# A hyperbolic transformer block on one core: one period per quad, joint scalar chains, tiles placed by the planner, one-bank PSUM tiles, other bias products

## The chip, the cores and the metric

One core of a Trainium2 chip. The metric is the device time of one launch in microseconds, median of the runs. Engines are named as in the profile: PE (TensorE), DVE (VectorE), ACT (ScalarE), POOL (GpSimd) and SP (SyncE, which here issues every DMA).

## The reference, cut to what matters

x is 128 x 64 x 256 in float32, cond is 128 x 256. A block of hyperbolic attention and a hyperbolic MLP are applied to x and the result is added to x. log0 and exp0 scale a row by a function of its norm; plin is exp0(log0(x) @ w + b).

```python
ada = t_emb @ w_ada + b_ada
sh_msa, sc_msa, g_msa, sh_mlp, sc_mlp, g_mlp = jnp.split(ada, 6, axis=-1)
xm = expmap0(layer_norm(logmap0(x)) * (1 + sc_msa) + sh_msa)
q = _to_heads(plin(xm, w_q, b_q))          # k, v alike; 16 heads of 16
attn = softmax(logmap0(q) @ logmap0(k).T / sqrt(HD))
attn_out = plin(_from_heads(expmap0(attn @ logmap0(v))), w_o, b_o)
x1 = mobius_add(x, expmap0(g_msa * logmap0(attn_out)))
xm = expmap0(layer_norm(logmap0(x1)) * (1 + sc_mlp) + sh_mlp)
ff = plin(plin(xm, w_f1, b_f1), w_f2, b_f2)
out = x + mobius_add(x1, expmap0(g_mlp * logmap0(ff)))
```

## The kernel before, in words

The 8192 rows are 64 tiles of 128 rows; four tiles are a quad, two a pair. Since log0 and exp0 only scale rows, the kernel never forms them: it carries rows and, per row, scalar factors, which are worked out on small tiles of 4, 8 or 16 columns (`norm_scalars`, `mobius_scalars`, `clip_factor`, `rsqrt_core`, L563 to L679): a long chain of tiny DVE operations with a few ACT logarithms and exponentials in between. The two MLP products have no activation between them, so `load_rest` (L748) folds the weights once into `wm`, two 256 x 256 blocks: f1 times f2 ("hw"), and f1 times its own transpose ("hm"), which gives the norm of the hidden row.

*Attention* (L983) runs over the quads of a group. `modulated` (L809) scales rows (on ACT or DVE, whichever is free), multiplies by the condition's scale on DVE, adds its shift on POOL (L819), and sums squares on ACT. `transposed` (L827) turns the rows on PE and spreads the inverse norms across partitions with four more transposes. `attention_pair` (L857) then takes a pair: q, k, v products (L868), bias products with one-row operands (L874), squares (L878) and their sums by head (L880), factors, scaled u and ve (L900, L904), transposes of u, qx and kT (L920, L924), 32 score products, exponentials in two pieces of 1024 columns (L936), 128 value products, division, transposes, and the product with wo (L976), whose bias comes as a full 128 x 512 product (L977). `gated` (L845) multiplies by the gate and sums squares and dot products. At the end of the group `mobius_scalars` works out two factors per row, a and b, and x1 = a x + b p is formed by one ACT or POOL and one DVE operation per tile (L1005, L1006).

*The MLP* (L1010) does the same for a group's quads: statistics, scalars, `modulated`, `transposed`, hm and hw, `fm` = hw times a factor plus b2 on DVE (L1062), `gated`, `mobius_scalars`, and the output with x added (L1076, L1077), stored per quad.

*The order of the work.* Groups are [0], [1, 2], ..., [13, 14], [15]: two quads share one run of each scalar chain. Nothing is issued as it is written: each operation goes into a `Plan` with an engine (or a choice, "ACT/DVE"), a modelled duration and a key: the quad's number for attention, plus `LAG` = 3.5 for its MLP (L1103). `Plan.run` (L150) sorts out an order by key and readiness, with its own durations, and `issue` writes it down; each engine then runs its list in that order. A DVE operation with SBUF inputs alone isn't picked while POOL is taken to be busy (L214). Where PE would have nothing to do, filler products of the identity are put in (`warm`, L1082). PSUM is two one-bank tiles ("bank") and three two-bank tiles ("dbl"). Row statistics of later quads are taken in four batches from x loaded for that alone (`passing`, L1096).

SP's queue issues all DMAs: x, the condition's scale, shift and gate rows per pair (written to DRAM once, read back with each row repeated 64 times), xr (x again, for the last addition) and the output.

## Time and profile before

| what | value |
|---|---|
| median of 3 runs | 911.72 us (911.11 to 917.18) |
| profiled execution, span | 919.3 us (its own time; no separate time of it is listed) |
| mean granted TensorE clock | 0.905 |
| PE, DVE, ACT, POOL busy | 814.0, 724.2, 501.6, 97.1 us |
| instructions | 24167 |
| DMA | 92.14 MB, mean 100 GB/s |
| first and last q product of attention | 27.55 us and 776.62 us from the span's start |

The page's first part gives each engine's busy time over the span, the second the same in 40 slices of 23 us. A table of stretches gives busy time by engine, the granted clock and DMA for any piece of the span. A group's line gives engine, operation, tiles (without numbers), shape and count, then busy time, mean length of one in ns, and the idle time ahead of it with what ended it. A float32 product is two matmul records, a transpose one. An engine starts an operation before the last one's record has ended, so a mean is some 0.08 to 0.11 us longer than the spacing of such operations in a dense run, and the groups' busy times add up to more than the engine's.

### The profile page before, as it was taken

What the parts mean: (1) busy time and instruction counts of PE and PEld (TensorE: products, weight loads), DVE (VectorE), ACT (ScalarE), POOL (GpSimd) and SP (SyncE); (2) the same over time, 40 slices, a digit from 0 to 9 for tenths busy, and PEclk for the clock granted to TensorE, in tenths of its full rate; (3) what the DMA queues carried; (4) which work ended last, traced back from release to release, by engine and by line L of the source; (5) the groups of instructions that cost most, each with busy time, mean ns of one, the idle gap of its engine ahead of it and who ended that gap; (6) DMA issues with size and microseconds to landing.
All of it is one profiled execution on the core that took longest, in us unless ns stands there. A gap on an engine that the chain in (4) does not pass through costs nothing.

```text
span 919.3 us, 24167 instructions
## 1 busy us (share of the span) xinstructions
PE 814.0 (89%) x9236; PEld 577.4 (63%) x9236; DVE 724.2 (79%) x2923; ACT 501.6 (55%) x1480; POOL 97.1 (11%) x91
## 2 busy tenths in 40 slices
PE   7888889898897988899879996999699959998996
PEld 5463556566676756676557764776477636766666
DVE  5567698758868997499966988689957996689877
ACT  2143455537765765457754774557646655555432
POOL 0002111000211111012010112021110111011200
PEclk9979979899989996799897996899879989999988
DMA  6886524102422425114441336024421251002413
GB/s 184 264 241 170 145 86 121 50 13 81 129 80 71 128 80 149 48 49 126 128 115 33 108 81 184 14 77 126 139 64 31 70 155 49 25 24 83 126 53 109
DMA packets 77268, 92.14 MB, mean 100 GB/s; under 512 B 7136, under 2 KB 59232, under 8 KB 77152
## 3 DMA queue, kind: packets, MB, share of 16 engines
q1 hardware_dynamic: 77152, 90.60, 34.8%
q8 instruction: 72, 1.18, 0.5%
q14 instruction: 44, 0.36, 0.1%
HBM read 81.40 MB, written 9.18 MB: 99 GB/s over the span
## 4 chain that ended last, share of the span: by engine, by line
PE 42%; DVE 29%; ACT 13%; issue 9%; DMA 5%; POOL 1%; SPq 1%; DVEq 0%; POOLq 0%; ACTq 0%
PE hmm L432 8%; PE ava L432 6%; PE wpa L432 5%; PE qka L432 5%; PE hwm L432 5%; PE tqa L436 3%; PE vva L432 3%; PE sca L432 2%; DVE bx L382 2%; DVE hs L395 2%; DVE p L382 2%; DVE ua L372 2%; PE wt L1084 1%; PE tza L436 1%; DMA mdm<-ada_d 1%
## 5 line engine op out<-in xcount | busy, mean ns | idle before, releaser
L432 PE MATMUL qka<-wqkv,yTa 128*128 128x512 f32 x256 | 144.6, 648 | 3.0 <-DVE maden L372 2.2
L432 PEld LDWEIGHTS vva<-wqkv,yTa 128*128 128x128 f32 x256 | 51.5, 203 | 72.9 <-issue 62.6
L432 PEld LDWEIGHTS ava<-ve,pta 64*64 64x64 f32 x4096 | 75.9, 157 | 18.4 <-issue 6.0
L432 PE MATMUL vva<-wqkv,yTa 128*128 128x256 f32 x256 | 81.0, 400 | 3.0 <-DVE n1st L410 1.5
L432 PE MATMUL ava<-ve,pta 64*64 64x17 f32 x4096 | 79.3, 223 | 1.8 <-issue 1.7
L1084 PE MATMUL wt<-ident 128*128 128x128 f32 x388 | 68.4, 322 | 5.0 <-ACT j1a L420 3.2
L432 PE MATMUL hmm<-wm,yTm 128*128 128x256 f32 x256 | 69.2, 417 | 1.1 <-ACT yTm L406 1.1
L432 PE MATMUL wpa<-wo,zTa 128*128 128x256 f32 x256 | 64.8, 398 | 5.2 <-ACT zTa L406 5.0
L420 ACT ACTIVATE usqa<-qka 128x1024 f32<-128x1024 f32 x32 | 32.4, 1014 | 67.2 <-PE vva L432 59.2
L436 PE MATMUL tqa<-ident,ua 128*128 128x128 f32 x256 | 44.1, 326 | 27.5 <-DVE ua L372 22.5
L1084 PEld LDWEIGHTS wt<-ident 128*128 128x128 f32 x388 | 57.2, 204 | 17.3 <-PE wt L1084 8.8
L420 ACT ACTIVATE qxa<-tqa,par 128x512 f32<-128x512 f32 x64 | 43.7, 687 | 43.0 <-PE tqa L436 31.0
L420 ACT ACTIVATE pta<-sca 128x1024 f32<-128x1024 f32 x64 | 62.6, 1019 | 8.2 <-PE sca L432 8.2
L375 POOL TENSOR_TENSOR ym<-ym,mdm 128x512 f32<-128x512 f32 x31 | 41.9, 1358 | 231.1 <-DVE ym L372 120.9
L432 PE MATMUL hwm<-wm,yTm 128*128 128x256 f32 x256 | 63.4, 390 | 0.0
L375 POOL TENSOR_TENSOR ya<-ya,mda 128x512 f32<-128x512 f32 x30 | 40.5, 1359 | 206.1 <-DVE ya L372 95.4
L432 PE MATMUL sca<-qxa,kTa 32*64 32x128 f32 x2048 | 44.5, 300 | 17.9 <-DVE ua L372 7.1
L432 PEld LDWEIGHTS hmm<-wm,yTm 128*128 128x128 f32 x256 | 50.0, 205 | 14.9 <-issue 6.9
L432 PEld LDWEIGHTS qka<-wqkv,yTa 128*128 128x128 f32 x256 | 50.6, 208 | 13.0 <-issue 4.1
L432 PEld LDWEIGHTS wpa<-wo,zTa 128*128 128x128 f32 x256 | 47.5, 196 | 15.9 <-ACT zTa L406 5.9
L436 PEld LDWEIGHTS tqa<-ident,ua 128*128 128x128 f32 x256 | 35.3, 167 | 31.9 <-issue 16.8
L432 PEld LDWEIGHTS hwm<-wm,yTm 128*128 128x128 f32 x256 | 46.2, 189 | 13.5 <-issue 8.4
(278 smaller groups left out, 1783.3 us busy)
## 6 DMA issues: line engine op xcount, KB each, us to landing
mda<-ada_d SPq DMA_DIRECT2D x64, 256.0 KB, 4.3
mdm<-ada_d SPq DMA_DIRECT2D x64, 256.0 KB, 4.1
x<-in_x_dram SPq DMA_DIRECT2D x16, 512.0 KB, 3.9
xr<-in_x_dram SPq DMA_DIRECT2D x32, 256.0 KB, 3.4
gaa<-ada_d SPq DMA_DIRECT2D x64, 128.0 KB, 3.1
gmm<-ada_d SPq DMA_DIRECT2D x64, 128.0 KB, 3.0
out_dram<-p SPq DMA_DIRECT2D x16, 512.0 KB, 3.8
xp<-in_x_dram SPq DMA_DIRECT2D x30, 256.0 KB, 3.3
```

The lines of the kernel that those rows point to most:

```text
L372: fn = lambda: self.nc.vector.tensor_tensor(out, a, b, op)
L375: fn2 = lambda: self.nc.gpsimd.tensor_tensor(out, a, b, op)
L382: fn = lambda: self.nc.vector.scalar_tensor_tensor(out, a, s, b, op0, op1, **({} if accum is None else {"accum_out": accum}))
L395: fn = lambda: self.nc.vector.tensor_reduce(out, a, AX.X, ALU.add)
L420: fn = lambda: self.nc.scalar.activation(out, a, func, scale=scale, **kw)
L432: fn = lambda: self.nc.tensor.matmul(out, lhsT=lhsT, rhs=rhs, start=start, stop=stop)
L436: self.add([("PE", lambda: self.nc.tensor.transpose(out, a, ident), 0.112, 0.2, False)], [a, ident], [out])
L1084: nc.tensor.matmul(wt[:, 0:P], lhsT=ident, rhs=ident, start=True, stop=True)
```

## The change

The kernel is written anew around the same arithmetic.

- One quad is the unit. `joined(q)` works out one Mobius chain of 8 columns for the attention of quad q and the MLP of quad q-2; `norms(q)` one normalisation chain for the MLP of quad q and the attention of quad q+3, whose x is loaded then and kept, so the loads for the statistics alone go.
- Every stage of a quad has a name, and its key is the quad's number times a step plus an offset from a table of about 130 (`OFF`). The planner, `arrange`, has other durations and also chooses the place of every tile (`SLOTS` lists tags and how many places each has). Every operation has one engine: all copies out of PSUM, the first normalisation scale and half of the x1 update go to ACT; POOL adds all shifts but the first quad's, multiplies by the scale in attention (half of the multiplications) and takes the rest of the x1 update, so x1 is ACT (b times p), POOL (a times x) and POOL (sum); the last quad's sum stays on DVE.
- PSUM is eight one-bank tiles: q/k per tile of rows, four score tiles with exponentials of 512 columns, two value tiles.
- Bias products: the inverse norms sit in one transposable tile, so a stage needs one transpose for them, not four; q/k and v biases are products with 4-row operands ahead of the main products, three to a pair; the MLP's are two of 512 columns with 4 rows (hm) and, for hw with b2, two with 8 rows, which replaces `fm`: hw's factor `ft` is put into the scalars instead. The bias of wo is four 128 x 128 transposes of a broadcast column.
- hm uses the symmetry of its weights: the second half of the rows is multiplied into 128 columns only, with a doubled block.
- At the start, weights of the MLP and x of quads 0 to 4 are loaded ahead of the condition, and the weights are folded before the first attention; quad 0 takes scale and shift by a selecting product (`pick`), without the trip through DRAM.

The diff, cut to its core:

```diff
-    GROUPS = [[0]] + [[q, q + 1] for q in range(1, NQ - 1, 2)] + [[NQ - 1]]
-    def bank(name):
-        return pl.tile(ps, [P, 512], "bank", name, 2, space="psum")
-    def dbl(name):
-        return pl.tile(ps, [P, 1024], "dbl", name, 3, space="psum")
+    pl.tag("bank", 8, (P, 512), ps, False)
+SLOTS = [
+    ("x", 5, (1024,)), ("ya", 3, (512,)), ("ym", 4, (512,)), ("mda", 2, (1024,)), ("mdm", 2, (1024,)),
...
+X1_ACT, OUT_POOL, MUL_POOL = (0, 1, 2, 3), (), ("a0", "a1")
+OFF = {
+    "asq1": -202327, "mmul1": -198589, "a1za0": -177714, "a0hsv": -160580, "x": -157317, "xr": -153864,
...
+STEP = 37000
+def key_of(name, q):
+    return q * STEP + OFF.get(name, 0)
...
+    def side(self, products, reserve=()):
...
+            for out, lhsT, rhs, start, stop in products:
+                self.nc.tensor.matmul(v(out), lhsT=v(lhsT), rhs=v(rhs), start=start, stop=stop)
...
     def modulated
-            pl.ts(y[:, t, :], src[:, t, :], s[:, t : t + 1], o[:, t : t + 1], ALU.mult, ALU.add, eng="ACT/DVE")
-            pl.tt(y[:, hs_, :], y[:, hs_, :], md[:, :, D : 2 * D], ALU.mult)
-            pl.tt(y[:, hs_, :], y[:, hs_, :], md[:, :, 0:D], ALU.add, eng="DVE/POOL" if i0 < 4 else "POOL")
+                pl.ts(y[:, t], src[:, k], s[:, k : k + 1], o[:, k : k + 1], ALU.mult, ALU.add, eng=ACT)
+                pl.tt(y, y, md[:, :, D : 2 * D], ALU.mult, eng=POOL if m + str(r) in MUL_POOL and q else DVE)
+                pl.tt(y, y, md[:, :, 0:D], ALU.add, eng=POOL if q else DVE)
...
     def attention_pair
-                (0, qk, 0, 0, 512, True), (1, qk, 32, 0, 512, True), (0, vv, 64, 512, 768, False), (1, vv, 64, 512, 768, True)
-                pl.mm(o_[:, t], rT[r : r + 1, t0 + t, :], bqkv[r : r + 1, n0:n1_], False, stop)
+        pl.side(
+            [(qk[t], rT[32 * t : 32 * t + 4], brow[32 * t : 32 * t + 4, t0 + t], True, False) for t in range(2)]
+            + [(vv.flat(), rT[64:68], brow[64:68].flat()[:, t0 * D : (t0 + 2) * D], True, False)],
...
-        pl.copy(kT.rearrange("p t f s -> p (t f s)"), tq[:, 512:1024], eng="DVE/ACT")
+        pl.copy(kT.flat(), tk.flat(), eng=ACT)
...
-            pl.mm(wps.rearrange("p t d -> p (t d)"), first, bo, False, True)
+                    pl.mm(wps[:, t, c * P : (c + 1) * P], boc[:, c : c + 1].wide(0, P)[:, :, 0], ident, t == c == 0, False, True)
...
+    def joined(q):
...
+        a, b = mobius_scalars(x2, wp, xpd, "mo", fts.get(q - 2), lo)
...
-            pl.ts(ax, x_q[:, i % 4, :], a[:, i : i + 1], None, ALU.mult, eng="ACT/POOL")
-            pl.stt(x1[:, i % 4, :], x1[:, i % 4, :], b[:, i : i + 1], ax, ALU.mult, ALU.add)
+                pl.ts(ax, x_q[:, t], a[:, t : t + 1], None, ALU.mult, eng=POOL)
+                if t in X1_ACT and q < NQ - 1:
+                    pl.ts(x1[:, t], x1[:, t], b[:, t : t + 1], None, ALU.mult, eng=ACT)
+                    pl.tt(x1[:, t], x1[:, t], ax, ALU.add, eng=POOL)
...
     def mlp
-                                pl.mm(o_[t], yT[:, c, t * P : (t + 1) * P], wm[:, c, m * D : (m + 1) * D], c == t0 == 0, False)
+                    pl.mm(hm[r][:, t], yT[r][:, 0, t], wm[:, 0, 0:D], False, False)
+                    pl.mm(hm[r][:, t, P:D], yT[r][:, 1, t], wm[:, 1, P:D], False, t == 1)
...
-                    pl.stt(f[:, t, :], hw[tt_], fh[:, tt_ : tt_ + 1], b2, ALU.mult, ALU.add)
+        pl.side([(hw[r].flat(), rT2[64 + 32 * r : 72 + 32 * r], mrow(r, 1, 8).flat(), False, True) for r in range(2)])
...
-    LAG = 3.5
-    batches = {0: (1, 3), 1: (3, 5), 3: (5, 10), 7: (10, 16)}
+    for q in range(NQ):
+        attention(q)
+        joined(q)
+        norms(q)
+        mlp(q)
+    joined(NQ)
+    joined(NQ + 1)
```

## The prediction

> **What bounds the kernel now.** I read the busy shares first, then the chain, then a table of 50 us stretches (two quads take about 100 us), then the groups, and last the timeline where a POOL instruction lies over DVE ones.

> ```profile
> PE 814.0 (89%) x9236; PEld 577.4 (63%) x9236; DVE 724.2 (79%) x2923; ACT 501.6 (55%) x1480; POOL 97.1 (11%) x91
> ...
> PE 42%; DVE 29%; ACT 13%; issue 9%; DMA 5%; POOL 1%; SPq 1%; DVEq 0%; POOLq 0%; ACTq 0%
> ```

> No engine is full over the span, and the chain changes hands between PE and DVE. The stretches say why. Their columns: stretch, length, busy us of PE, PEld, DVE, ACT and POOL with counts, granted TensorE clock, DMA share, GB/s.

> ```profile
> 410.00:460.00 50.00, 46.48 (x506) 32.14 (x505) 46.36 (x202) 36.15 (x112) 7.14 (x6) 0.93 0.45 135
> 460.00:510.00 50.00, 43.34 (x591) 31.91 (x590) 33.73 (x115) 25.99 (x70) 4.87 (x5) 0.83 0.25 67
> 510.00:560.00 50.00, 46.48 (x324) 30.84 (x322) 45.63 (x191) 35.62 (x119) 8.26 (x7) 0.96 0.42 116
> 560.00:610.00 50.00, 43.75 (x771) 33.04 (x772) 34.88 (x130) 23.75 (x57) 3.26 (x4) 0.80 0.24 66
> 610.00:660.00 50.00, 46.96 (x328) 31.34 (x327) 47.73 (x190) 34.76 (x116) 9.39 (x8) 0.97 0.40 117
> ```

> Every other stretch is full of DVE work (46.4, 45.6, 47.7 of 50 us: 93%), and between them DVE has 34 us while PE works at a clock of 0.80 to 0.83. So a quad costs 50 us though DVE has only (46.4 + 33.7 + 45.6 + 34.9)/4 = 40.2 us for it. A schedule that mixes the two kinds of stretch evenly could be shorter with the same work.

> ```profile
> L432 PE MATMUL wpa<-bo,first 128*128 128x512 f32 x64 | 32.7, 592 | 0.0
> L382 DVE SCALAR_TENSOR_TENSOR x<-x,mab,ax 128x256 f32<-128x256 f32 x64 | 29.2, 495 | 2.3 <-ACT ax L361 1.3 <-POOL ax L354 1.0
> L382 DVE SCALAR_TENSOR_TENSOR fm<-hwm,fh,b 128x256 f32<-128x256 f32 x64 | 28.3, 476 | 0.4
> L404 DVE COPY zTa<-tza 128x256 f32<-128x256 f32 x32 | 12.7, 419 | 38.9 <-PE tza L436 35.0 <-ACT zTa L406 3.9
> L375 POOL TENSOR_TENSOR ya<-ya,mda 128x512 f32<-128x512 f32 x30 | 40.5, 1359 | 206.1 <-DVE ya L372 95.4 <-PE wpa L432 12.7 <-DVE cht L382 12.2
> ```

> These are rows that the change removes, or (the last) multiplies. The price of the last shows in the timeline (start, length):

> ```profile
> 419.48 0.42 DVE L382 SCALAR_TENSOR_TENSOR j3m<-x,p 128x256 f32<-128x256 f32 x1
> 419.71 1.31 POOL L375 TENSOR_TENSOR ya<-ya,mda 128x512 f32<-128x512 f32 x1 [8.79 <-DVE ya L372]
> ...
> 420.16 1.14 DVE L382 SCALAR_TENSOR_TENSOR j3m<-x,p 128x256 f32<-128x256 f32 x1
> ```

> The second j3m takes 1.14 us where the first took 0.42: it ends 0.28 us after POOL does. DVE operations with two SBUF inputs stand still beside a POOL one; those with an input in PSUM (ua, za) and BATCH_NORM keep their length. Summed over all DVE rows, the excess over each row's median beside a POOL instruction is 30.4 us for 85 POOL instructions: 0.36 us each.

> **The change, part by part.** Counts are those of the order in which the built program's instructions stand; from the fourth quad on it repeats with every quad (161 DVE instructions), with attention and MLP work side by side. An instruction costs its spacing in a dense run: a row's mean less about 0.08 us on DVE, 0.09 to 0.11 on ACT.

> *DVE, per quad.* Before, dense spacings and counts without start-up and statistics give 37.7 us, plus 30.4/16 = 1.9 of stall: 39.6. The eight stretches from 410 to 810 show 40.7 busy, 1.03 times that. Taken away: the residual update x<-x,mab (4 x 0.40), the scaling fm (4 x 0.40), the copies zT, kT, yT and rT (87 in all, 2.8 per quad), the first normalisation's scale (38, 0.8), and half of the multiplications of y (33 x 0.60 / 16 = 1.2): 8.0. Added: four half-size reductions for two (0.1); the statistics of the quad three ahead (4 BATCH_NORM of 0.33, 1.3), which before lie outside these stretches; and scalar operations: two norm and Mobius chains per quad where there were three per two quads, with the new factors some 22 more at 0.08 (1.8; a chain of 8 columns costs per operation what one of 4 does). 37.7 - 8.0 + 3.2 = 32.9; my count of the whole after-list gives 33.0.

> *POOL, per quad.* 5.6 additions or multiplications of 512 (1.36), 4 ax (0.58), 3.75 additions of 256. No row shows the last; it lies between ax (0.58) and the 512 row (1.36), and by size at 0.68, half the latter. Sum 7.6 + 2.3 + 2.6 = 12.5 us and 13.4 instructions, against 6 us before. Stall of DVE: at the least nothing (POOL beside PSUM operations only), at the most POOL's whole 12.5 us, as the j3m row shows for one instruction. By time the old ratio gives 12.5 x 30.4/97 = 3.9, by count 13.4 x 0.36 = 4.8: I take 4.4, since the operations are the same kinds. DVE then needs 37.4; its busy time was 1.03 times such a sum before, so 38.5.

> [...]

> *PE, per quad.* Dense runs at full clock: q, k and v of a pair 5.25 us, their bias rows 1.07, transposes 0.11 each, scores 1.16, values 1.95, output product with bias 2.59, an MLP half product 2.45 with bias rows. A quad comes to 39.2. Changes: output bias 0.86 to four transposes of 0.11 (-0.9 for two pairs); one half-size block of the symmetric MLP product left out (-1.1); 3 transposes of inverse norms for 8 (-0.55); bias rows -0.3 in attention and -0.7 in the MLP. No row shows four-row bias products: if three row groups run side by side, as the four one-row products did in 1.07, a pair costs 0.86; if not, 2.6, which would be 5 us a quad. I take 0.9, since the rows nearest to them overlap. With two filler products: 36.1.

> *ACT, per quad.* All PSUM copies, the normalisation scale and b times x1 now go there: 24 squares x 0.51, 8 exponentials of 512 (taken at the 512 row's 0.48), 6 squares of 512 x 0.48, 8 scales x 0.49, 4 qx x 0.59, copies 4.4, b 3.75 x 0.41, small 2.6 = 33.8, up from 474/16 = 29.6. It stays below DVE and hides there; the third rival is what it costs if it does not.

> *The ends.* Before, the first q product stands at 27.55 us and the last ends at 778; 142 us of tail follow. After, x, all MLP weights and five quads of x are issued ahead of the condition: about 5.6 MB, at the first slices' 184 to 264 GB/s some 24 us, then the ada product (3.75 us), which SP waits for because the second half of w_ada takes the first's tile, then 1.75 MB more (8 us) and landing (3): first q product at about 42. In exchange the fold of the weights, 66 to 90 us before, lies in this gap, as does the quad-0 modulation without its trip through DRAM. The tail: after the last qkv PE has 68 us of work against 101 (120 fillers of 0.22 in each); the old proportion gives 95, the bare chain of one quad (attention 24, scalars and output of both halves 46) gives 70; I take 85. From a quad's first to its last qkv, 10.

> *DMA and SP.* 349 issues for 384; the 30 statistics loads go. 84 MB in 740 us is 113 GB/s, within what the stretches show (135); mda and mdm keep two tiles, and their 4.3 us landing lies inside a 20 us half-period.

> **Sum.** One period P: DVE's 38.5 us at the 93% which the full stretches reach is 41.4. PE needs 36.1/0.93 = 38.8, ACT 33.8. Span: 42 + 15 x 41.4 + 10 + 85 = 758. The profiled span before (919.3) lies 0.8% above the median of the runs (911.7), so 752 as a median.

> **The rivals.**
> 1. POOL meets only PSUM operations: the planner's list puts them beside it. Then DVE needs 34, PE's 38.8 is the period: 137 + 582 = 719, or 713. For it: ua, ve, za, gates, reductions and BATCH_NORM, which POOL does not stop, are 16 us a quad. Against: the old planner kept the same rule and lost 30 us.
> 2. The stall costs POOL's whole time: (33.0 + 12.5) x 1.03/0.93 = 50.4, span 893, median 886. For it: longer rows beside POOL (1.14). Against: the measured third. Half-way (8.5) gives P 46, 827, median 820.
> 3. The period is not filled, because ACT's queue holds PSUM copies behind squares (two of 0.51): 13 copies at up to 1 us on PE's 36 give 46 to 49; 820 and up to 865. Against: ACT was idle 45% of the time.
> [...]
> 5. It does what it says but not evenly: the old 81% filling (40.7 of 50) gives P 47.5, 850, median 843.

> **How the numbers follow.** Forecast (710 to 800) 0.60; rival 1 and better 0.16; rivals 2, 3 and 5 together 0.19, most of it at 800 to 850; rival 4 0.05. The range 690 to 825 leaves out about a tenth on each side. A difference under 1% can't be told from none in this kernel: faster 0.94, same 0.02, slower 0.04.

> **What would show it.** Right: DVE busy near 93% in the middle slices with no alternation, POOL about 210 us busy, a stall of 60 to 80 us in the SBUF rows of DVE, PE clock at 0.93 or more, first qkv near 42 us, quads 41 us apart. Wrong: quads 46 us apart or more, idle of PE named after ACT, a clock under 0.85, bias products over 1 us a pair.

## The result, and the profile after

The changed kernel takes 796.17 us (median of 4 runs, 795.37 to 801.29) against 912.26 us for the kernel before (4 runs): ratio 0.873, 95% interval 0.8693 to 0.8766. The profiled execution took 796.09 us, its span is 794.3 us. Medians, here and below, are over all runs of a kernel; a ratio is over those within 1.5% of its shortest, and the kernel before ran again beside each set of experiments.

The page of the changed kernel: busy shares, the granted clock in 40 slices, the chain.

```profile
PE 764.6 (96%) x9032; PEld 538.8 (68%) x9032; DVE 606.0 (76%) x2934; ACT 526.5 (66%) x1770; POOL 203.3 (26%) x240
...
PEclk9999999998969889797979899797989899998899
...
PE 74%; DVE 15%; ACT 6%; issue 1%; DMA 1%; POOL 1%; SPq 0%; POOLq 0%; DVEq 0%; ACTq 0%
```

The chain no longer changes hands: 74% of it is PE, which had 42%, and PE has work 96% of the time. But the clock row dips to 7 again and again. The same 50 us stretches as were read before (columns: stretch, length, busy PE, PEld, DVE, ACT, POOL, clock, DMA share, GB/s):

```profile
300.00:350.00 50.00, 49.60 (x575) 35.55 (x573) 40.29 (x195) 37.83 (x135) 15.45 (x17) 0.90 0.45 122
350.00:400.00 50.00, 49.61 (x567) 34.26 (x566) 38.69 (x195) 36.32 (x122) 15.29 (x16) 0.90 0.40 107
400.00:450.00 50.00, 49.20 (x687) 34.33 (x685) 39.03 (x218) 37.05 (x124) 14.47 (x17) 0.90 0.41 107
450.00:500.00 50.00, 49.61 (x616) 33.67 (x613) 38.59 (x187) 37.22 (x129) 16.08 (x20) 0.84 0.41 112
```

The alternation is gone: every stretch is alike, with DVE at 39 of 50 us (78%) and PE at 49.5, at a clock of 0.84 to 0.90. The groups that answer to those shown of before (busy us, mean ns, idle ahead of it):

```profile
L686 PE MATMUL bank<-ident,boc 128*128 128x128 f32 x128 | 20.0, 278 | 0.0
L632 POOL TENSOR_TENSOR x<-x,ax 128x256 f32<-128x256 f32 x60 | 42.4, 727 | 3.4 <-ACT x L622 3.3
L659 ACT ACTIVATE zT<-bank 128x256 f32<-128x256 f32 x64 | 20.8, 377 | 9.5 <-PE bank L686 9.3
L632 POOL TENSOR_TENSOR ya<-ya,mda 128x512 f32<-128x512 f32 x60 | 76.8, 1282 | 91.0 <-ACT ya L624 60.3 <-DMA mda<-ada_d 23.9 <-DMA ga<-ada_d 4.5
```

**Where the 125 us between the two spans came from.** From the records of PE and of the clock: between its first and last record PE idles 95.4 us before and 24.2 after (-71.2); the clock is at half speed for 175.5 us of the span before and 139.9 after, of which half is lost if PE works throughout (-17.8); the rest, PE's work at full clock with its fillers and the 10 and 5 us ahead of its first record and behind its last, is 736 and 700 us (-36).

**A spell in every quad.** From the sixth quad (233.1 us) to the thirteenth, quads start 44.4 us apart (for example at 321.8, 366.2, 410.7, 455.1, 499.5), and the clock falls to half in each: from 272.7 to 539.0 us every spell is 10.24 us long and they too are 44.4 us apart. All spells of the span are 3.41, 6.83 or 10.24 us long, and they start whole multiples of 3.41 us apart, so in this trace the clock changes on a grid of 3.41 us. The stretches of that length about one spell:

```profile
399.02:402.43 3.41, 3.41 (x83) 2.92 (x81) 3.41 (x35) 2.23 (x11) 0.00 (x0) 1.00 0.57 162
402.43:405.85 3.42, 3.02 (x74) 1.90 (x72) 2.27 (x20) 3.42 (x11) 1.96 (x3) 1.00 0.02 5
405.85:409.26 3.41, 3.41 (x72) 2.31 (x70) 2.28 (x6) 3.18 (x13) 3.14 (x6) 0.50 0.38 114
409.26:412.67 3.41, 3.41 (x11) 1.49 (x6) 3.38 (x22) 1.60 (x8) 0.00 (x0) 0.50 0.76 212
412.67:416.09 3.42, 3.42 (x8) 1.92 (x8) 2.02 (x10) 0.60 (x1) 0.00 (x0) 0.50 0.36 72
```

PE was busy 3.02 of 3.42 us (88%) in the stretch ahead of the spell, and all the time inside it. Ahead of the spell at 586.75 us it had no idle time at all:

```profile
583.34:586.75 3.41, 3.41 (x122) 2.21 (x114) 1.90 (x6) 3.41 (x11) 3.15 (x6) 1.00 0.25 84
586.75:590.17 3.42, 3.42 (x12) 1.61 (x7) 3.39 (x18) 2.69 (x15) 1.15 (x2) 0.50 0.42 134
```

In the kernel before, a spell follows a real gap; the line below is the stretch ahead of the one at 559.5 us:

```profile
556.04:559.46 3.42, 1.91 (x16) 1.28 (x13) 2.81 (x8) 2.58 (x7) 1.30 (x1) 1.00 1.03 302
```

So what was PE doing at 402 us? Its timeline (start, length; the operand's rows stand first in "rows*columns"):

```profile
402.58 0.30 PE L686 MATMUL bank<-ident,iva 128*128 128x128 f32 x1
403.01 0.49 PE L1429 MATMUL bank<-ident 128*128 128x128 f32 x2
403.76 0.30 PE L686 MATMUL bank<-ident,ivw 128*128 128x128 f32 x1 [0.27 <-DVE mob L638]
403.99 1.12 PE L689 MATMUL bank<-ve,pt 64*64 64x17 f32 x64
405.05 1.33 PE L709 MATMUL bank<-brow,rTw 8*128 8x512 f32 x4
406.30 1.91 PE L689 MATMUL bank<-ve,pt 64*64 64x17 f32 x64
408.14 2.08 PE L709 MATMUL bank<-brow,rTa 4*128 4x512 f32 x6
```

Value products with 64 of 128 rows, bias products with 4 and 8. I worked out for each 3.41 us stretch the streaming time of its products (0.85 ns for each column of a record, their spacing in dense runs), each weighted by its active rows over 128. Over the 394 full-clock stretches of both traces, a border at 0.36 of a stretch sorts those followed by half clock (39 in the two traces) from the others with 3 on the wrong side; the best border on PE's unweighted busy share leaves 24 there. The stretch at 402.43 has 0.31, those inside the spell 0.16, 0.33 and 0.50, after which the clock is full again.

### The profile page after: what moved, and what is told of

It is laid out like the page before. It is cut to its first block, busy times and chain, and to the rows that moved or that the text cites. A ratio compares the mean times of both kernels' runs of the same rounds, so it can differ in the third digit from the quotient of the medians.

```text
span 794.3 us, 24205 instructions
## 1 busy us (share of the span) xinstructions
PE 764.6 (96%) x9032; PEld 538.8 (68%) x9032; DVE 606.0 (76%) x2934; ACT 526.5 (66%) x1770; POOL 203.3 (26%) x240
## 3 DMA queue, kind: packets, MB, share of 16 engines
q8 instruction: 71, 1.16, 0.6%
## 4 chain that ended last, share of the span: by engine, by line
PE 74%; DVE 15%; ACT 6%; issue 1%; DMA 1%; POOL 1%; SPq 0%; POOLq 0%; DVEq 0%; ACTq 0%
PE bank L689 53%; PE bank L709 11%; PE bank L686 9%; DVE jd L638 3%; ACT ja L675 2%; PE bank L1429 2%; DVE mok L638 1%; DMA mdm<-in_L_cond_w_f_dram 1%; ACT ym L624 1%; ACT pt L675 1%; DVE u L630 0%; DMA x<-in_x_dram 0%; DVE moy L630 0%; DVE bx L638 0%; SPq L722 0%
## 5 line engine op out<-in xcount | busy, mean ns | idle before, releaser
L689 PE MATMUL bank<-wqkv,yTa 128*128 128x512 f32 (+1 forms) x512 | 207.6, 556 | 0.0
L689 PEld LDWEIGHTS bank<-wqkv,yTa 128*128 128x128 f32 x512 | 106.9, 217 | 84.0 <-issue 77.5
L632 POOL TENSOR_TENSOR ym<-ym,mdm 128x512 f32<-128x512 f32 x30 | 39.2, 1311 | 298.7 <-DVE ym L630 260.9
L689 PE MATMUL bank<-wm,yTm 128*128 128x256 f32 (+1 forms) x512 | 108.7, 365 | 1.9 <-ACT yTm L659 1.8
L689 PEld LDWEIGHTS bank<-wm,yTm 128*128 128x128 f32 x512 | 89.2, 195 | 22.6 <-issue 9.1
L689 PEld LDWEIGHTS bank<-ve,pt 64*64 64x64 f32 x4096 | 73.8, 149 | 29.5 <-issue 24.7
L650 DVE TENSOR_REDUCE hs<-usq 128x32 f32<-128x512 f32 x96 | 64.7, 679 | 25.7 <-ACT usq L675 25.6
L675 ACT ACTIVATE pt<-bank 128x512 f32<-128x512 f32 x128 | 72.7, 600 | 16.2 <-PE bank L689 16.1
L689 PE MATMUL bank<-ve,pt 64*64 64x17 f32 x4096 | 80.2, 218 | 0.7 <-ACT pt L675 0.6
L615 POOL TENSOR_SCALAR ax<-x,moa 128x256 f32<-128x256 f32 x64 | 36.3, 578 | 143.4 <-DVE mob L638 70.0
L1429 PE MATMUL bank<-ident 128*128 128x128 f32 x384 | 69.4, 333 | 3.6 <-POOL ident masks.py:199 1.4
L689 PE MATMUL bank<-wo,zT 128*128 128x256 f32 x256 | 60.6, 379 | 0.0
L630 DVE TENSOR_TENSOR u<-bank,gg 128x512 f32<-128x512 f32 x64 | 42.7, 685 | 0.6
```

The lines of the kernel that those rows point to most:

```text
L615: fn = lambda: self.nc.gpsimd.tensor_scalar(v(out), v(a), v(s1), 1.0, op0, ALU.mult)
L630: self._dve(lambda: self.nc.vector.tensor_tensor(v(out), v(a), v(b), op), out.size, [a, b], [out])
L632: fn = lambda: self.nc.gpsimd.tensor_tensor(v(out), v(a), v(b), op)
L650: self._dve(lambda: self.nc.vector.tensor_reduce(v(out), v(a), AX.X, ALU.add), a.size, [a], [out], 0, False)
L675: self.nc.scalar.activation(v(out), v(a), func, scale=v(scale), **kw)
L689: fn = lambda: self.nc.tensor.matmul(v(out), v(lhsT), v(rhs), start=start, stop=stop)
```

## The experiments

**Theories.** *R* (formed from the result): the clock follows active rows; the low stretch holds the clock at half once a quad, costs half of 10.2 us, and PE's 39.3 us at full clock becomes 44.4. *B*: the clock follows PE's busy time, so gaps must be at fault. *D*, the prediction's own: DVE's work and its stall beside POOL set the period.

**1. Bias products with 32 rows.** The rows of zeros that lie beside the 4 or 8 used ones are multiplied too; nothing else changes.

```
-  (qk[t], rT[32 * t : 32 * t + 4], brow[32 * t : 32 * t + 4, t0 + t], True, False)
+  (qk[t], rT[32 * t : 32 * t + 32], brow[32 * t : 32 * t + 32, t0 + t], True, False)
...
-  (hw[r].flat(), rT2[64 + 32 * r : 72 + 32 * r], mrow(r, 1, 8).flat(), False, True)
+  (hw[r].flat(), rT2[64 + 32 * r : 96 + 32 * r], mrow(r, 1, 32).flat(), False, True)
```

> The bias products take 32 rows instead of 4 or 8; the added rows are zeros on both sides, so they take the same time. Theory R (the clock counts streaming time weighted by active rows; a stretch of 3.41 us under about 0.37 is followed by half clock): the stretch ahead of each spell rises from 0.31 to about 0.36, the first stretch in the spell from 0.16 to 0.27 and the second from 0.33 to 0.41, so a spell of 10.2 us becomes one of 6.8 us or goes: quads 39.3 to 42.7 us apart instead of 44.4, 720 to 770 us. Rival B (the clock counts the time in which PE is busy, whatever the rows) and rival D (DVE with POOL's stall sets the period): nothing changes, 790 to 802 us.

Measured: 745.04 us, ratio to before 0.8185 (0.8135 to 0.8235): 6.4% under the changed kernel by the times, 6.2% by the two ratios. Its clock row on the page, and a stretch that lies over a quad's products as the one at 402.43 did (0.09 us earlier), with the next:

```profile
PEclk9999999999999999999999999999999999999899
```

```profile
538.60:542.01 3.41, 3.02 (x75) 1.95 (x73) 2.36 (x21) 3.41 (x11) 1.87 (x3) 1.00 0.02 4
542.01:545.42 3.41, 3.41 (x76) 2.03 (x75) 2.92 (x9) 3.41 (x14) 3.23 (x6) 1.00 0.42 115
```

PE is busy for the same 3.02 us, the weighted share is about 0.41 for 0.31 (the 0.09 us of transposes account for 0.03 of it), and the clock stays at 1.00. Quads stand 39.6 us apart, and no spell is left before the tail. B and D fall: zeros were added, no gap was closed and no work of DVE taken away.

**2 and 3. The same time on PE, with 128 rows and with 4.** Three more products of 128 columns ahead of the first values product of each pair, once with all rows of the identity, once with four.

```
             with pl.group([z]):
+                if k == 0:
+                    pl.open["fn"] += [lambda b=av[0]: pl.filler(pl.ap(b.flat()))] * 3
```

In the second kernel `pl.fill4` stands for `pl.filler`, with `lhsT=idp[0:4], rhs=idp[0:4]`.

> Three 128-row products of 128 columns (0.22 us each) more ahead of the first values product of each pair, into a bank that the values then overwrite; the order is kept. Theory R: the low stretch rises from 0.31 to about 0.5, the spells go, PE needs 39.3 + 1.3 = 40.6 us a quad: 796 - 15 x 3.8 = 739 us, up to 760 if some spells stay. Rivals B (PE was busy there already, the time only grows) and D: 796 to 816 us.

> The same three products at the same place, but with 4 rows instead of 128: the same time on PE. Theory R: 4 rows add next to nothing to the low stretch, the spells stay and the work gets longer: 796 to 825 us. Rival B: as with 128 rows, so the same time as that kernel, whichever it is.

Measured: 775.02 us (four runs from 767.78 to 785.82; ratio 0.8446, 0.8381 to 0.8511; the profiled run took 780.8) with 128 rows, 820.72 us (0.8998, 0.8934 to 0.9062) with 4. The three products in the timeline (six records, since a float32 product is two), first kernel, then the second:

```profile
408.85 0.83 PE L1431 MATMUL bank<-ident 128*128 128x128 f32 x6
```

```profile
353.31 0.93 PE L1432 MATMUL bank<-ident 4*128 4x128 f32 x6
```

They take nearly the same time and differ in their rows, and the medians differ by 46 us; the shortest run with 4 rows (814.81) is 29 us above the longest with 128. With 128 rows half clock lasts 64.0 us of the profiled span, with 4 rows 143.4. That is R against B. With 128 rows the time was over R's forecast of 739, and over its 760: two spells of 3.41 us per quad stayed until 449 us, behind stretches under the border (0.34 at 397.6 and at 411.3 us) on either side of the one with the fillers, with quads 44.2 us apart; after that the rhythm slips and quads are 40.9 us apart, near the 40.6 that R has for no spells.

**4. Sixteen rows.** As experiment 1, with 16 for 32.

> The bias products with 16 rows instead of 32. Theory R, as a question of dose: the low stretch ahead of a spell rises only from 0.31 to 0.335, the first in the spell from 0.16 to 0.21, the second from 0.33 to 0.37; spells stay, some of them 6.8 us instead of 10.2: 765 to 796 us, between 4 and 32 rows. If any more rows than 8 were enough: 745 us.

Measured: 788.22 us (768.78 to 789.22), against 914.98 before on that chip. The profile is that of the shortest run: 78.8 us at half clock, where the changed kernel has 139.9 and the 32-row one 13.0. The dose lies in between, as R has it.

**5 and 6. More work for DVE.** POOL's multiplications of y are issued on DVE (in the changed kernel); then all of y's multiplications and additions (in the 32-row kernel).

```
-                pl.tt(y, y, md[:, :, D : 2 * D], ALU.mult, eng=POOL if m + str(r) in MUL_POOL and q else DVE)
+                pl.tt(y, y, md[:, :, D : 2 * D], ALU.mult, eng=POOL if m + str(r) in MUL_POOL and q else DVE, on=nc.vector)
```

(`on` changes the engine that is issued to, not the planner's order.)

> The multiplications of y that POOL does (two of 512 columns a quad) go to DVE at the same places of the order. DVE gets 2 x 0.6 = 1.2 us a quad more, POOL 2.6 us less. Rival D (the prediction's step: DVE's work and its stall set the period): the period grows by 0.4 to 0.9 us, 802 to 810 us. Theory R: DVE is idle 20% of a quad's time, so the period stays at 44.4 us: 790 to 802 us.

> With 32-row bias products, and all multiplications and additions of y that POOL does issued on DVE at the same places of the order: DVE gets 5.6 x 0.60 = 3.4 us a quad more and loses part of its stall; its busy time goes from 34.4 to about 37.5 us of 39.6. Rival D (the prediction's rule that DVE can be filled to 93%): the period becomes 37.5/0.93 = 40.3 us or more, 755 to 775 us. If PE alone is the bound as long as DVE has any idle time: 740 to 750 us.

Measured: 795.34 us (0.874, 0.8694 to 0.8785), quads 44.4 us apart: nothing. And 752.54 us (0.8231, 0.8189 to 0.8274): 1% over the 32-row kernel, between the two forecasts. Stretches of the second:

```profile
350.00:400.00 50.00, 49.46 (x662) 34.67 (x655) 47.10 (x230) 40.55 (x141) 7.07 (x12) 1.00 0.49 130
400.00:450.00 50.00, 49.47 (x689) 34.39 (x688) 44.33 (x211) 36.23 (x123) 5.05 (x8) 0.93 0.39 106
```

In the first DVE is busy 47.1 of 50 us, and PE idles no more than in the 32-row kernel (25.9 and 26.5 us in all). Quads without a spell are 39.8 us apart with DVE busy for 37.3 us (94%), where most were 39.5 apart with DVE at 87%. Most of the 1% goes with spells that came back (51.2 us of half clock against 13.0), which neither theory had in its expectation. So DVE's work doesn't set the period of either kernel: 1.5 us more of it a quad cost nothing, 3 us some 0.3. D's rule that 93% is the limit is neither shown nor refuted: it gives 37.3/0.93 = 40.1 us here, too near to 39.8.

**7. All stage offsets at zero.** `OFF = {}`: the same instructions, taken quad by quad in program order. (It isn't the order of the kernel before, which had a planner too.)

> The changed kernel with all stage offsets at zero: the same instructions, but the planner takes them quad by quad in program order. If the searched order carries the gain (my theory: of the 125 us between the two profiled spans, 71 us are PE's idle time): PE idle rises to 80 us or more, half clock follows the gaps, 850 to 920 us. If the removed work on DVE, PE and the statistics' DMAs carries it: 800 to 840 us.

Measured: 893.81 us, 0.9766 (0.9706 to 0.9825).

```profile
PE 808.3 (90%) x9458; PEld 583.5 (65%) x9458; DVE 655.3 (73%) x2934; ACT 531.3 (59%) x1770; POOL 209.0 (23%) x240
```

PE idles for 79.8 us and has 213 more fillers (810 records for 384), which stand where it has nothing else to do: 213 x 0.22 = 47 us. 79.8 - 24.2 + 47 = 103 us, about the whole difference of the spans (896.4 and 794.3). Of the 116 us that the rewrite gains, 98 are gone without the searched offsets; less work in this order is worth 2.3% (1.8 to 2.9), 21 us. This is one other order; what a searched order would do for the kernel before was not tried. DVE's stall beside POOL is 55.5 us in this order, with the same instructions that lose 21.7 in the searched one.

**8 to 10. The wait for `u`.** In the changed kernel the MLP's two 4-row bias products run one after the other. PE's weight loads say why (waiting, released by: us, times, longest), and the timelines of PE and DVE, of the changed kernel, show one case:

```profile
PEld bank L709 <- DVE u L630: 7.3, 11, 0.7
```

```profile
395.01 2.15 PE L709 MATMUL bank<-brow,rTm 4*128 4x512 f32 x4
```

```profile
395.30 0.69 DVE L630 TENSOR_TENSOR u<-bank,gg 128x512 f32<-128x512 f32 x1
```

The second product's bank is still read by DVE's multiplication of u until 395.99; the product starts at 396.04. I took the two behind the first product group (with 32 rows), where the bank has long been free; then with three and with two full-row products in the low stretch.

```
-        pl.side([(hm[r].flat(), rT[64 + 32 * r : 96 + 32 * r], mrow(r, 0, 32).flat(), True, False) for r in range(2)])
+        late = pl.side(
+            [(hm[r].flat(), rT[64 + 32 * r : 96 + 32 * r], mrow(r, 0, 32).flat(), r == 1, r == 0) for r in range(2)], (), False
+        )
...
+                if r == 0:
+                    pl.open["fn"].append(late)
```

> With 32-row bias products, and the two bias products of the MLP's first half moved behind the first product group: that group opens its bank itself, and the bank of the second half has been released by DVE's multiplication of u by the time it is needed. The two products then run side by side, 1.0 us a quad where they took 2.06 one after the other. PE is at full clock and 99% busy, so each us that it saves shortens the period: 39.6 - 1.0 = 38.6 us apart, 745 - 15 = 730 us. Rival D (DVE with POOL's stall bounds the period now that the clock is full): no gain, 740 to 750 us. If the wait for u only moves to another bank: also no gain.

> The kernel with 32-row bias products and the moved MLP bias, and three full-row products of 128 columns ahead of the first values product of the first pair only, in the low stretch that still brought spells there (0.285 and 0.25 of a stretch). Theory R: 0.19 more lifts it to 0.45, no spells; PE needs 39.6 - 1.0 + 0.66 = 39.3 us: quads 39.3 us apart, 735 to 742 us, less spread between runs than without the products. If the spells came from something else than the low stretch: 750 to 760 us, as without them.

> The same with two products: 0.285 + 0.125 = 0.41, just over the border of 0.37 to 0.41. Quads 39.05 us apart without spells, 731 to 740 us; a spell now and then, up to 750.

Measured: 758.99 us (747.47 to 759.3; before 914.98; the profiled run took 759.3) without fillers, 748.59 (0.8215, 0.818 to 0.8249) with three, 745.32 (0.818, 0.8141 to 0.8218) with two. The products do run side by side (last kernel), in 1.06 us of PE's spacing instead of 2.06. All three lie above R's forecasts (730, 735 to 742, 731 to 740). PE is then early at the next step:

```profile
416.02 1.13 PE L709 MATMUL bank<-brow,rTm 32*128 32x512 f32 x4
```

```profile
421.76 0.30 PE L686 MATMUL bank<-ident,iva 128*128 128x128 f32 x1 [0.51 <-ACT che L675]
```

Half of the us becomes a wait for the inverse norms, 5.7 us on, and it falls in the low stretch: without fillers that stretch drops to 0.285 and spells come back (54.1 us of half clock). With fillers they go (13.7 and 22.8 us, in the tail but for two early ones), and the fillers cost what is left: quads 40.0 and 39.7 us apart. My gain of 1.0 us a quad was wrong: the wait moved.

**11. The 32-row kernel once more**, beside 9 and 10.

> 32-row bias products alone, once more beside the other two: 741 to 748 us.

Measured: 745.24 us, 0.8174 (0.8139 to 0.8208). With 10 it is the fastest version; the two are the same within the intervals.

**12. The kernel before with 32-row bias products**, the masked zeros in `bqkv` and `bm`.

```
-                pl.mm(o_[:, t], rT[r : r + 1, t0 + t, :], bqkv[r : r + 1, n0:n1_], False, stop)
+                pl.mm(o_[:, t], rT[r : r + 32, t0 + t, :], bqkv[r : r + 32, n0:n1_], False, stop)
```

> The kernel before, with its one-row bias products given 32 rows (31 of zeros) in the same order. There the stretches ahead of spells are low because PE waits: with the added rows 4 of 20 would rise, and only two of them past 0.41. Theory R: 0 to 10 us, 900 to 912 us. If few rows were what slows the kernel before too: 860 us or less.

Measured: 908.26 us, 0.9961 (0.9924 to 0.9998). Half clock still lasts 147.0 us of the span (175.5 before), so there gaps, not rows, bring most spells. The 6% that rows are worth belong to the changed kernel, where PE has few gaps left.

## Why the prediction was right or wrong

Forecast 752 us (690 to 825), measured 796: the sign and the range held, the mechanism that sets the period did not.

- **"One period P: DVE's 38.5 us at the 93% which the full stretches reach is 41.4"**: this step failed, twice over. DVE's own work of 33.0 us was right (34.4 busy in the 32-row kernel's 39.6 us, less its stall of 1.3). The stall was taken as 4.4 us a quad; the excess over the rows' medians beside POOL is 21.7 us, 1.4 a quad, 0.09 us per POOL instruction against 0.36 before. So rival 1's condition nearly came true, and its objection ("the old planner kept the same rule and lost 30 us") was no argument: experiment 7 shows the loss to be a matter of order, 55.5 against 21.7 us. And DVE didn't set the period at all: it was busy 78% of the middle stretches, and more work for it changed little (experiments 5 and 6); whether 93% is a limit of it stays open. POOL's whole time, 12.5 us a quad, was the most that the prediction thought could be lost; the trace of before has a third of POOL's time lost (30.4 of 97.1 us), that of after a ninth (21.7 of 203.3).
- **PE 36.1 us a quad**: 39.3 at full clock (44.4 less 5.1), and 39.6 in the 32-row kernel. There the pieces are, by PE's spacing: bias products 5.3 us for 3.6. The two sets of three for q, k and v take 1.08 each and run side by side, as taken (0.9); the MLP's first pair runs in series, 2.06. Fillers 0.8 for 0.44; values 4.2 for 3.9; idle time and longer transposes about u, iva and ivw 0.7. Together 3.1 of the 3.5 missing.
- **Half clock**: the sum has no term for it, and the chances have 0.05 (rival 4). In the trace before, every half-clock spell follows 3.41 us in which PE was busy 75% or less, but gaps were the wrong variable: in the trace after, ahead of the spells up to 713 us PE was busy 81 to 100% of the 3.41 us, ahead of the one at 586.75 us in all of it. The spells cost 5.1 us a quad. PE was busy for 96% of the span, where it had been for 89%, and the mean clock was 0.912 for 0.905, not "0.93 or more". So the period is rival 1's, with PE the bound (38.8), plus a regular half-clock spell that no case of the prediction had.
- **The sum**: 42 + 15 x 41.4 + 10 + 85 = 758; measured 41.8 + 632.0 + 20.6 + 99.9 = 794.3. The first four quads took 146.1 us, 19.5 less than 4 x 41.4, which I had not thought of: the first MLP product stands at 119.8 us. The other eleven took 485.9, 30.5 more. So part of the period's error was hidden by luck. From the last quad's first to its last qkv it was 20.6 us, not 10. In the tail, up to 10 of the missing 15 us are half of its spells' 20.
- **The profiled execution 0.8% above the median**: true of before; the profiled run after is at its median (796.09 and 796.17), which adds 6 us to the error.
- **Right**: the head (41.8 for 42), POOL 203 us for about 210 (the x1 sum 0.727 us for 0.68), ACT 32.9 us a quad for 33.8 and hidden, no alternation, DMAs hidden. Of its own signs of being right, four failed: DVE near 93% (78%), a stall of 60 to 80 us (21.7), a clock of 0.93 or more (0.912), quads 41 us apart (44.4).

The price of the order was not in the prediction at all. Experiment 7 puts it at 98 us of 116, against one unsearched order; the prediction had it only as even stretches.

## What to carry to other kernels

When PE is full and the granted clock still dips in a rhythm, list the active rows of the products in the 3.4 us ahead of each dip: here zero rows beside the used ones raised them at no cost in time and gave 6%. A full engine with a period that repeats exactly deserves suspicion: 44.4 us was 13 times 3.413, not the sum of anybody's work. A us saved on the bounding engine is only kept if what it waits for next is early too.
